# Four-layer graph network: six of sixteen neighbour lists made between layer 0's weighings, node products within the first lists, table rows of 520, anchored lists

## The chip, the cores and the metric

The kernel runs on one core of a Trainium2 chip. A core has a matrix engine (TensorE, in the profile PE, with its weight loads as PEld), three engines for elementwise work (VectorE or DVE, ScalarE or ACT, GpSimd or POOL), a synchronisation engine (SyncE, SP) that mainly issues transfers, and 16 DMA engines that all queues share. Each engine runs its instructions in order and waits for the others by semaphores. SBUF is the on-chip memory of 128 partitions, PSUM the accumulator of TensorE. The metric is the device time of one execution in microseconds; the times given are the median of runs without a profile.

## The reference

The input is x of 8 batches, 2048 nodes and 64 features, and one adjacency matrix for all batches, symmetric, with the diagonal set and some 9 entries in a row. Four layers each compute x = layernorm(x + layer(x, adj)). Cut to what matters here:

```python
# layer 0: graph attention with a LeakyReLU of a sum of two scores
h = layernorm((x * node_weights + node_bias + x) @ W) * gamma + beta
s1, s2 = h @ a1, h @ a2
e = leaky_relu(s1[:, :, None] + s2[:, None, :], 0.2)
att = softmax(where(adj > 0, e, NEG), axis=-1)
x = layernorm(x + elu(att @ h + h))
# layer 1: attention per feature, softmax of feat * wa over the neighbours
# layer 2: mean of the neighbours, two products, relu, layernorm
# layer 3: four dot-product attention heads over h = x Wh, then one over their joined output
```

Only about 9 of 2048 entries of each row count, so the kernel works on lists of edges.

## The kernel before, in words

Nodes are cut into 16 tiles of 128. A tile has NG = 2 groups of 64 nodes, and each group's edges are laid into GS = 5 slots of 128 places, filled from the group's two ends inwards: nodes 0 to 31 forwards, 32 to 63 backwards. WINDOWS (line 69) says which nodes of a group may have edges in which slot; since degrees are random, the windows overlap. For each tile the kernel makes `SelT` and `Sel` (which place belongs to which node, and its turn) and `src` (which node's row each place must fetch). A gather is one indirect DMA, issued by GpSimd, that fetches 128 rows of a table in DRAM by `src`; a tile takes ten (L204, helper `gather`).

**List phase** (the loop at L364 on). For each tile the adjacency rows are loaded by SP (`load`), turned into marks and counted on ScalarE (`on`, L368), for the first eight tiles also transposed by TensorE into ET (L376, L377); VectorE makes keys (L370), takes the largest eight of each 256 (L380), merges them to 24 neighbours (L385, L387); TensorE sums the degrees of the nodes in front (`before`, L396), VectorE makes offsets and, with ScalarE's `apart` (L405), `SelT` (L406); ten products and two copies make `Sel` (L411 to L415), seven instructions make `src` (L419 to L427). After each second list `node_products` does two tiles of h = x W: transposes (L127), products with W (L301) and with the attention vectors (L303), a square on ScalarE (L306), reduction (L307), an inverse root in some twelve small instructions (L142 to L147), the scaled H (L316). H stays in SBUF for all tiles and is stored to the table `htab0`, rows of 512 (8 batches x 64); a score stands in place of column 0 of W, which the sum of the others restores later. The order of this phase is set by the framework's scheduler.

**Weighing** (manual order, the loop over k that calls fetch, weights, divide, combine, weigh, activate, normalise). Step k gathers tile k+1 into `hs` (two buffers), adds the two scores (`wm`, L461), makes exponentials on ScalarE (L464, L465), multiplies the gathered rows by them (L476, five instructions), sums by node on TensorE (L482, with the denominators `pd`, L484), divides the tile before (`rd`, L490 and ScalarE, L493), and for the tile before that restores the column, applies gamma and beta and adds H (L497 to L500), then ELU and the residual (L502 to L508) and layer norm's statistics for pairs of tiles (L156 to L162); `normed` on ScalarE (L170) applies them.

Layer 1 begins with `f` on ScalarE (L580). Its lists, layer 2's and layer 3's use the same `Sel` and `src`. In layer 3's heads (manual order) a step is one slot of one group: ten gathers to a tile, scores of the slot's 128 rows against the window's nodes (L1101), exponentials (L1104), the edge mask (L1107), sums `po` (L1126). `sides` makes U, the node side of the scores, in two calls for a tile; ScalarE copies head h0 and VectorE head h0 + 1 (L1073, L1074).

Of the kernel before, what the change touches and what calls it, by code (L numbers as in the profile page):

```python
# [48 lines left out]
def kernel(ctx: ExitStack, tc: tile.TileContext, ins: dict, out: bass.AP):  # L49
# [19 lines left out]
    WINDOWS = [(0, 20), (10, 32), (20, 44), (32, 54), (44, 64)]  # L69
# [117 lines left out]
    room = main.tile([P, 2], F32, name="room")  # L187

# [35 lines left out]
    htab0 = dram.tile([N + 1, BD], F32, name="htab0")  # L224
    no_row(htab0)
    l0 = ExitStack()
    wp = l0.enter_context(tc.tile_pool(name="l0w", bufs=1, reuse_waits="tile"))
    H = wp.tile([P, NT, BD], F32, name="H")
# [4 lines left out]
    aps = adj_.enter_context(tc.tile_pool(name="adjps", bufs=2, space=PSUM, reuse_waits="tile"))  # L233
# [5 lines left out]

    ats = {0: load(0)}  # L240
    a1 = rows("a1", ins["L0_gnn_a"].rearrange("f o -> (f o)")[0:D], wp)
# [20 lines left out]
    for k, a in enumerate((a1, a2)):  # L262
# [5 lines left out]
        if k:  # L268
            first_col = wp.tile([P, 2], F32, name="first_col")
            nc.vector.tensor_copy(first_col, Wv[:, :, 0])  # L270
            nc.vector.tensor_copy(Wv[:, :, 0], Wa[:, 1])
            nc.vector.tensor_copy(Wa[:, 1], first_col)

# [13 lines left out]
    def node_products(t0, wk, ps):  # L287
# [4 lines left out]
        for q in range(HALF):  # L292
# [12 lines left out]
            sq = wk.tile([P, B, D], F32, name="sq")  # L305
            nc.scalar.activation(sq.rearrange("p b d -> p (b d)"), ph.rearrange("p a n -> p (a n)"), AF.Square)  # L306
            nc.vector.tensor_reduce(var[:, q], sq[:, :, 1:], AX.X, ALU.add)  # L307
            held.append(ph)
        v4, r4, t4 = (a.rearrange("p q (a k) -> p q a k", k=2) for a in (var, rstd, tmp))
        nc.vector.tensor_tensor(t4, pq[:, :, :, 1], pq[:, :, :, 1], ALU.mult)  # L310
        nc.vector.tensor_tensor(var, var, tmp, ALU.add)
        nc.vector.scalar_tensor_tensor(var, var, 1.0 / D, eps.unsqueeze(2).to_broadcast(var.shape), op0=ALU.mult, op1=ALU.add)
        inv_sqrt(*(a.rearrange("p q b -> p (q b)") for a in (rstd, var, tmp)))
        for q, ph in enumerate(held):
            t = t0 + q
            nc.vector.tensor_tensor(H[:, t].rearrange("p (b d) -> p b d", d=D),  # L316
                                    ph.rearrange("p a (k d) -> p (a k) d", d=D), along(rstd[:, q]), ALU.mult)
            nc.sync.dma_start(htab0[t * P:(t + 1) * P, :], H[:, t])
# [33 lines left out]
    base = aw.tile([P, 1], F32, name="base")  # L352
    nc.vector.tensor_scalar(base, part[:, 3:4], float(GB), float(GE), op0=ALU.is_ge, op1=ALU.mult)

# [9 lines left out]
    for it in range(NT):  # L364
        at = ats.pop(it) if it in ats else load(it)
        nc.scalar.dma_start(X[:, it], x[:, it * P:(it + 1) * P, :].rearrange("b p d -> p b d"))
        on = ap_.tile([P, N], BF16, name="on")
        nc.scalar.activation(on, at, AF.Sign, bias=minus_half, accum_out=deg[:, it:it + 1])  # L368
        key = ap_.tile([P, N], F16, name="key")
        nc.vector.tensor_tensor(key, on, from_end, ALU.mult)  # L370
        nc.vector.tensor_scalar(deg[:, it:it + 1], deg[:, it:it + 1], 0.5, 0.5 * N, op0=ALU.mult, op1=ALU.add)
        for c in range(NCH if it < DENSE else 0):
            pt = aps.tile([P, TPC, P], F32, name="pt")
            for k in range(TPC):
                j0 = (c * TPC + k) * P
                nc.tensor.matmul(pt[:, k], on[:, j0:j0 + P], ident_bf, start=True, stop=True)  # L376
            nc.scalar.activation(ET[:, c * TPC:(c + 1) * TPC, it * P:(it + 1) * P], pt, AF.Relu, saturate=False)  # L377
        tops = ap_.tile([P, N // SEG, 8], F16, name="tops")
        for k in range(N // SEG):
            nc.vector.max(tops[:, k], key[:, k * SEG:(k + 1) * SEG])  # L380
        topf = tops.rearrange("p k m -> p (k m)")

        nbr = ap_.tile([P, SL + 1], F16, name="nbr")
        for k in range(0, SL, 8):
            nc.vector.max(nbr[:, k:k + 8], topf)  # L385
            if k + 8 < SL:
                nc.vector.match_replace(topf, nbr[:, k:k + 8], topf, 0.0)  # L387
        junk = ap_.tile([P, P], BF16, name="junk")
        nc.vector.scalar_tensor_tensor(junk, on[:, it * P:(it + 1) * P], 1.0, ident_bf, op0=ALU.mult, op1=ALU.mult,
                                       accum_out=own_edge[:, it:it + 1])  # L390
        nc.vector.scalar_tensor_tensor(junk[:, 0:SL], nbr[:, 0:SL], 0.0, nbr[:, 0:SL], op0=ALU.is_gt, op1=ALU.logical_and,
                                       accum_out=listed[:, it:it + 1])

        plist = aps.tile([P, 2 * CW], F32, name="pl", bufs=1)
        poff = plist[:, 0:1]
        nc.tensor.matmul(poff, before, deg[:, it:it + 1], start=True, stop=True)  # L396
        nc.vector.tensor_scalar(offs[:, it:it + 1], poff, -1.5 * GE, 2.0 * GE, op0=ALU.max, op1=ALU.min)
        nc.vector.tensor_tensor(offs[:, it:it + 1], offs[:, it:it + 1], base, ALU.add)
# [6 lines left out]
        nc.scalar.activation(apart, node_half, AF.Abs, scale=2.0, bias=ends[:, it:it + 1])  # L405
        nc.vector.tensor_scalar(SelT[:, it], apart, deg[:, it:it + 1], None, op0=ALU.is_lt, saturate=False)  # L406
        pl = plist[:, 1:1 + GS * NG * (SL + 1)].rearrange("p (g l) -> p g l", l=SL + 1)
        ps = plist[:, CW // 2:CW // 2 + GE].rearrange("p (s n) -> p s n", n=P)
        for s in range(GS):
            sel = SelT[:, it, s * P:(s + 1) * P]  # L410
            nc.tensor.matmul(pl[:, s * NG:(s + 1) * NG], sel, nbrs, start=True, stop=True)  # L411
            nc.tensor.matmul(ps[:, s], sel, ident_h, start=True, stop=True)
        for k in range(GN // GB):
# [3 lines left out]
                                 AF.Copy, saturate=False)  # L417
        at_ = ap_.tile([P, GS, NG], F32, name="at_")
# [9 lines left out]
        if it % HALF == HALF - 1:  # L428
            node_products(it - HALF + 1, ap_, aps)
    adj_.close()  # L430
# [4 lines left out]
    wk = l0.enter_context(tc.tile_pool(name="l0k", bufs=2, reuse_waits="tile"))  # L435
    ps_e = l0.enter_context(tc.tile_pool(name="l0pse", bufs=2, space=PSUM, reuse_waits="tile"))
    ps_o = l0.enter_context(tc.tile_pool(name="l0pso", bufs=3, space=PSUM, reuse_waits="tile"))
    ps_w = l0.enter_context(tc.tile_pool(name="l0psw", bufs=1, space=PSUM, reuse_waits="tile"))
    held, zs, stats = {}, {}, {}

    def fetch(it):
        hs = wk.tile([P, GS * NG, B, D], F32, name="hs")
        for s in range(GS):
            for g in range(NG):
                gather(hs[:, s * NG + g].rearrange("p b d -> p (b d)"), htab0, it, s, g)
        selTf = wk.tile([P, GE], F32, name="selTf")
# [6 lines left out]
        pe = ps_e.tile([P, GS, NG * B], F32, name="pe")  # L453
        for s in range(GS):
            nc.tensor.matmul(pe[:, s], selTf[:, s * P:(s + 1) * P], s1g.rearrange("p g b -> p (g b)"), start=True, stop=True)  # L455
        held[it] = hs, self_, pe

    def weights(it):
        hs, self_, pe = held[it]
        wm = wk.tile([P, GS * NG, B], F32, name="wm")  # L460
        nc.vector.tensor_tensor(wm, pe.rearrange("p s (g b) -> p (s g) b", b=B), hs[:, :, :, 0], ALU.add)  # L461
# [4 lines left out]
        held[it] = hs, self_, w, wm  # L466

    def weigh(it):
        hs, self_, w, wm = held[it]
        po = ps_o.tile([P, BD], F32, name="po")  # L470
        pd = ps_w.tile([P, B], F32, name="pd")
        for n, ss in enumerate(TOGETHER):
            for s in ss:
                own = slice(s * NG, (s + 1) * NG)
                wx = hs[:, own].rearrange("p g b d -> p (g b) d")
                nc.vector.tensor_tensor(wx, wx, along(w[:, own].rearrange("p g b -> p (g b)")), ALU.mult)  # L476
# [10 lines left out]
    def divide(it):  # L487
# [4 lines left out]
        for b in range(B):  # L492
            nc.scalar.activation(z[:, b], z[:, b], AF.Copy, scale=rd[:, b:b + 1])  # L493
# [1678 lines left out]
```

## Time and profile before

| | us |
|---|---|
| median of 3 runs (1674.72 to 1679.46) | 1674.98 |
| the profiled execution, its own time | 1810.59 |
| its span in the profile | 1808.8 |

Busy time by stage of the profiled execution, in us (the stages' limits are read from the timeline):

| stage | from, to | TensorE | VectorE | ScalarE | GpSimd | clock | DMA share |
|---|---|---|---|---|---|---|---|
| lists and node products | 0, 182 | 98.4 | 149.5 | 106.0 | 4.1 | 0.69 | 0.44 |
| first gathers | 182, 200.5 | 4.4 | 0.4 | 1.0 | 11.7 | 0.50 | 0.60 |
| weighing | 200.5, 452.9 | 133.5 | 195.5 | 105.1 | 141.5 | 0.68 | 0.53 |
| layer 1 | 452.9, 712 | 224.3 | 157.2 | 111.4 | 134.5 | 0.94 | 0.54 |
| layer 2 | 712, 955 | 177.3 | 150.6 | 127.2 | 128.5 | 0.87 | 0.44 |
| layer 3, heads | 955, 1446 | 447.9 | 321.0 | 274.1 | 169.3 | 0.98 | 0.56 |
| layer 3, last attention | 1446, 1808 | 292.6 | 221.7 | 180.7 | 193.4 | 0.87 | 0.58 |

The clock is the share of full speed that TensorE was granted; DMA share is the mean busy share of the 16 DMA engines. In rows of groups the numbers are busy time, mean ns of one, then idle time of the engine just before and what ended it. In a timeline a row has its start, length, engine, line, operation and shapes, and in brackets the idle time before it with what ended it.

### The profile page before, as it was taken

To read this page: it belongs to the slowest core of one execution; us is meant where nothing else is said; L and a number is where in the kernel's file an instruction comes from. 1 tells how busy PE (TensorE), PEld (TensorE's weight loads), DVE (VectorE), ACT (ScalarE), POOL (GpSimd) and SP (SyncE) were. 2 spreads that over 40 slices of the span, in tenths; PEclk is the share of its full clock that TensorE was granted. 3 is DMA by queue.
4 is the path that set the end of the run, shared out by engine and by line. 5 is a ranking of instruction groups with operands and counts; after the bars stand their busy time and mean duration, and the time that the engine had idled before them with its cause. 6 is when DMAs were issued, how large, how long until landed. Compare 5 with 4: busy or idle time off the path is not lost.

```text
span 1808.8 us, 39940 instructions
## 1 busy us (share of the span) xinstructions
PE 1378.3 (76%) x16028; PEld 949.9 (53%) x16028; DVE 1195.8 (66%) x2973; ACT 905.6 (50%) x1863; POOL 782.8 (43%) x777
## 2 busy tenths in 40 slices
PE   4673455653489996888937999999999779889993
PEld 3662233331133332732216777777777657667773
DVE  5989378787576465754763666666667626656667
ACT  5763133535961233535653556555655424555564
POOL 0000666662464552656624333334334056656551
PEclk9665667666799998999967999999999969998897
DMA  6550665552126883256614656665656266666651
GB/s 185 184 160 24 182 179 175 174 175 60 70 105 214 305 309 126 94 153 177 184 46 119 160 155 164 161 160 156 170 155 165 76 198 171 186 179 176 182 152 44
DMA packets 157019, 280.71 MB, mean 155 GB/s; under 512 B 68732, under 2 KB 94332, under 8 KB 154748
## 3 DMA queue, kind: packets, MB, share of 16 engines
q0 software_dynamic: 56320, 189.44, 35.5%
q1 hardware_dynamic: 83866, 84.45, 15.8%
q10 hardware_dynamic: 16640, 4.20, 1.0%
q8 instruction: 128, 2.10, 0.5%
q14 instruction: 65, 0.53, 0.1%
HBM read 237.60 MB, written 40.42 MB: 154 GB/s over the span
## 4 chain that ended last, share of the span: by engine, by line
PE 48%; ACT 8%; DVE 7%; issue 5%; DMA 1%; another core or an unknown queue 1%; POOL 1%; SPq 0%; ACTq 0%; POOLq 0%; DVEq 0%
PE pscore L1101 9%; PE pa L605 6%; PE po L1126 5%; PE ps L1429 5%; PE po L1468 4%; PE pt L1406 3%; PE pa L660 2%; PE pt L713 2%; ACT w L1104 2%; PE pa L1003 2%; PE pscore L1064 2%; PE py L833 2%; PE pe L1399 2%; PE pscore L1193 2%; ACT xsT L1088 1%
## 5 line engine op out<-in xcount | busy, mean ns | idle before, releaser
L204 POOL DMA_INDIRECT xs<-xtab,src x160 | 172.9, 1081 | 282.0 <-PE po L1126 243.9
L204 POOL DMA_INDIRECT hs<-htab,src x160 | 153.1, 957 | 261.7 <-PE pe L455 182.9
L204 POOL DMA_INDIRECT hs<-ktab,src x160 | 158.6, 992 | 139.4 <-DMA utab<-hT 46.3
L605 PE MATMUL pa<-R,ET 128*128 128x512 bf16 x768 | 179.4, 390 | 49.9 <-POOL R L593 33.7
L1107 DVE SCALAR_TENSOR_TENSOR w<-w,Sel 128x640 f32<-128x640 f32 (+2 forms) x160 | 134.2, 875 | 104.7 <-ACT w L1104 104.5
L1104 ACT ACTIVATE w<-pscore 128x640 f32<-128x640 f32 (+2 forms) x160 | 113.6, 745 | 145.5 <-PE pscore L1101 139.9
L1101 PE MATMUL pscore<-U,xsT 64*128 64x80 f32 (+2 forms) x2560 | 163.6, 278 | 5.4 <-DVE U L1074 4.3
L605 PEld LDWEIGHTS <-ET 128*128 128x128 fp8e4 x768 | 74.7, 100 | 162.5 <-issue 83.3
L170 ACT ACTIVATE X<-X,ln_m,ln_r 128x64 f32<-128x64 f32 x256 | 87.2, 427 | 144.3 <-DVE ln_m L162 134.0
L1101 PEld LDWEIGHTS pscore<-U,xsT 64*128 64x128 f32 x2560 | 152.6, 191 | 11.6 <-DVE U L1074 6.9
L1126 PE MATMUL po<-w,xs 128*64 128x88 f32 (+2 forms) x3072 | 130.8, 237 | 14.4 <-DVE w L1107 5.3
L1126 PEld LDWEIGHTS po<-w,xs 128*64 128x64 f32 x3072 | 113.8, 139 | 48.0 <-DVE w L1107 25.6
L1468 PE MATMUL po<-hs,w 128*32 128x65 f32 x2048 | 87.3, 234 | 33.2 <-issue 25.3
L1429 PE MATMUL ps<-U,hsT 128*128 128x64 f32 x768 | 104.3, 287 | 9.0 <-ACT hsT L1407 4.8
L1429 PEld LDWEIGHTS ps<-U,hsT 128*128 128x128 f32 x768 | 102.8, 210 | 10.0 <-ACT hsT L1407 5.4
L204 POOL DMA_INDIRECT rs<-rtab,src x80 | 75.8, 948 | 63.4 <-PE pa L660 43.0
L614 DVE RECIPROCAL rec<-pa 128x256 f32<-128x256 f32 x32 | 54.4, 1734 | 64.6 <-PE pa L660 30.8
L1468 PEld LDWEIGHTS po<-hs,w 128*32 128x32 f32 x2048 | 70.8, 118 | 45.0 <-issue 33.4
L1407 ACT COPY hsT<-pt 128x512 f32<-128x512 f32 x96 | 52.5, 586 | 81.8 <-remote 46.4
L476 DVE TENSOR_TENSOR hs<-hs,w 128x1024 f32<-128x1024 f32 x80 | 91.8, 1213 | 1.2 <-ACT wm L464 0.4
L204 POOL DMA_INDIRECT rs<-ytab,src x80 | 76.9, 961 | 32.9 <-issue 17.1
L1516 ACT ACTIVATE z<-z,ln_m,ln_r 128x64 f32<-128x64 f32 x240 | 83.4, 432 | 14.7 <-DVE ln_m L1504 14.1
(634 smaller groups left out, 3087.4 us busy)
## 6 DMA issues: line engine op xcount, KB each, us to landing
at<-in_adj SPq DMA_DIRECT2D x16, 1024.0 KB
R<-itab SPq DMA_DIRECT2D x60, 256.0 KB
rtab<-r SPq DMA_DIRECT2D x16, 512.0 KB
ptab<-hp SPq DMA_DIRECT2D x16, 384.0 KB
hi<-ptab SPq DMA_DIRECT2D x16, 384.0 KB
ktab<-hb SPq DMA_DIRECT2D x16, 260.0 KB
X<-in_x ACTq DMA_DIRECT2D x16, 256.0 KB
htab<-H SPq DMA_DIRECT2D x16, 256.0 KB
```

Source lines behind the costliest of these rows:

```text
L170: nc.scalar.activation(v[:, b], v[:, b], AF.Identity, scale=rstd[:, k:k + 1], bias=nmr[:, k:k + 1])
L204: nc.gpsimd.indirect_dma_start(out=dst, out_offset=None, in_=table[:, :], in_offset=bass.IndirectOffsetOnAxis(ap=src[:, it, s, g:g + 1], a ...
L476: nc.vector.tensor_tensor(wx, wx, along(w[:, own].rearrange("p g b -> p (g b)")), ALU.mult)
L605: nc.tensor.matmul(po[h].rearrange("p a f -> p (a f)"), ET[:, jt, it * P:(it + 1) * P], R[:, jt, q, h].rearrange("p a f -> p (a f)"), star ...
L614: nc.vector.reciprocal(rec, po[h][:, 0])
L1101: nc.tensor.matmul(pscore[:, k_, f0:f0 + HN * ni].rearrange("p (h i) -> p h i", i=ni), xsT[half, p], Us[it][half, p, :, i0:i0 + ni], start ...
L1104: nc.scalar.activation(w.rearrange("p k a h i -> p k (a h i)"), pscore[:, :, 0:NP * HN * ni], AF.Exp)
L1107: nc.vector.scalar_tensor_tensor(wt, wt, 3.0e38, edge, op0=ALU.min, op1=ALU.mult)
L1126: nc.tensor.matmul(po[half, p, :, a - blk * GB:b - blk * GB], xs[:, f0:f0 + D], w[:, k_, p, :, a - WINDOWS[s][0]:b - WINDOWS[s][0]], start ...
L1429: nc.tensor.matmul(pscore[:, g, 2 * p:2 * p + 2], hsT[:, g, p], U[:, p, :, node_block(g, k)], start=False, stop=(p == NP - 1))
L1468: nc.tensor.matmul(po[node_block(g, k), j, b], w[:, g, t], hs[:, g, t], start=(s == BEGIN[k] and b == 0), stop=(s == END[k] and b == B // ...
L1516: nc.scalar.activation(v, v, AF.Identity, scale=r, bias=n)
```

## The change

The lists of tiles 0 to 9 are made first, as before; those of tiles 10 to 15 are cut into small parts (`mark`, `count`, `make_keys`, `top_of`, `neighbours`, `tests`, `places`, `select`, `edges`, `sources`), which `between` puts into the weighing's steps 0 to 12, one list in two steps. All node products come with the first eight lists, two tiles with each, and x is loaded two tiles to a list. The table's rows grow to 520: eight scores stand behind the 512, so that column 0 needs no restoring. GpSimd multiplies H by gamma before it is stored, and adds beta for a second table `own0`, from which SP loads a tile's own rows again in the weighing. `hs` gets three buffers, `combine` follows one step behind. Lists are anchored: two more masks (`far`) and shifts give nodes from 16 and from 28 on, counted from a group's ends, a least place of 128 and 256, so that the windows are 16, 18, 32, 18 and 16 wide instead of 20, 22, 24, 22 and 20; the offset is the maximum of three sums. In layer 3 the middle slot's weights have a buffer of their own, and U is copied by halves of the batches.

```diff
-    WINDOWS = [(0, 20), (10, 32), (20, 44), (32, 54), (44, 64)]
+    ANCHORS = (16, 28)
+    WINDOWS = [(0, 16), (10, 28), (16, 48), (36, 54), (48, 64)]
...
-    htab0 = dram.tile([N + 1, BD], F32, name="htab0")
+    htab0 = dram.tile([N + 1, BD + B], F32, name="htab0")
+    own0 = dram.tile([N, BD], F32, name="own0")
...
-            nc.vector.tensor_reduce(var[:, q], sq[:, :, 1:], AX.X, ALU.add)
+            nc.vector.tensor_reduce(var[:, q], sq, AX.X, ALU.add)
...
-        nc.vector.tensor_tensor(t4, pq[:, :, :, 1], pq[:, :, :, 1], ALU.mult)
-        nc.vector.tensor_tensor(var, var, tmp, ALU.add)
...
-            nc.vector.tensor_tensor(H[:, t].rearrange("p (b d) -> p b d", d=D),
-                                    ph.rearrange("p a (k d) -> p (a k) d", d=D), along(rstd[:, q]), ALU.mult)
-            nc.sync.dma_start(htab0[t * P:(t + 1) * P, :], H[:, t])
+            H = wk.tile([P, BD + B], F32, name="H")
+            Hv = H[:, 0:BD].rearrange("p (b d) -> p b d", d=D)
+            nc.vector.tensor_tensor(Hv, ph.rearrange("p a (k d) -> p (a k) d", d=D), along(rstd[:, q]), ALU.mult)
+            nc.vector.tensor_tensor(H[:, BD:].rearrange("p (a k) -> p a k", k=2), pq[:, q, :, 1], r4[:, q], ALU.mult)
+            nc.gpsimd.tensor_tensor(Hv, Hv, over(g0, Hv.shape), ALU.mult)
+            nc.sync.dma_start(htab0[t * P:(t + 1) * P, :], H)
+            Hb = wk.tile([P, B, D], F32, name="Hb")
+            nc.gpsimd.tensor_tensor(Hb, Hv, over(b0, Hv.shape), ALU.add)
+            nc.sync.dma_start(own0[t * P:(t + 1) * P, :], Hb.rearrange("p b d -> p (b d)"))
...
+        for k in range(3):
+            nc.tensor.matmul(poff[:, k:k + 1], ident_bf, shift_bf[:, k:k + 1], start=True, stop=False)
+            nc.tensor.matmul(poff[:, k:k + 1], outer[k], deg[:, it:it + 1], start=False, stop=True)
...
+        nc.vector.tensor_reduce(far_off, poff, AX.X, ALU.max)
+        nc.vector.tensor_scalar(offs[:, it:it + 1], far_off, 2.0 * GE, depth[:, 1:2], op0=ALU.min, op1=ALU.mult)
...
-        if it % HALF == HALF - 1:
-            node_products(it - HALF + 1, ap_, aps)
+    AHEAD = 10
+    for it in range(AHEAD):
+        for t in range(2 * it + 2, min(2 * it + 4, NT)):
+            load_x(t)
...
+        if it < NT // HALF:
+            node_products(it * HALF, prk, prps)
+    products.close()
...
-        hs = wk.tile([P, GS * NG, B, D], F32, name="hs")
+        hs = rk.tile([P, GS * NG, BD + B], F32, name="hs", bufs=3)
...
+    def prepare(it):
+        own = wk.tile([P, B, D], F32, name="own")
+        nc.sync.dma_start(own.rearrange("p b d -> p (b d)"), own0[it * P:(it + 1) * P, :])
...
     def combine(it):
-        z = zs[it]
-        nc.vector.tensor_tensor(z, z, H[:, it].rearrange("p (b d) -> p b d", d=D), ALU.add)
-        nc.vector.tensor_reduce(z[:, :, 0], z[:, :, 1:], AX.X, ALU.add, negate=True)
-        nc.vector.tensor_tensor(z, z, over(g0, z.shape), ALU.mult)
-        nc.vector.tensor_tensor(z, z, over(b0, z.shape), ALU.add)
+        z, own = zs[it]
+        nc.vector.tensor_tensor(z, z, own, ALU.add)
...
+    def between(k, place_):
+
+        it, odd = AHEAD + k // 2, k % 2
+        if it < NT:
+            if (odd, place_) == (0, 3):
+                mark(it)
+            if (odd, place_) == (0, 2):
+                count(it)
+                make_keys(it)
+                top_of(it, 0, 4)
+            if (odd, place_) == (1, 0):
+                top_of(it, 4, N // SEG)
+            if (odd, place_) == (1, 1):
+                neighbours(it)
+                tests(it)
+                places(it)
+            if (odd, place_) == (1, 2):
+                select(it)
+                edges(it)
+        if (odd, place_) == (0, 0) and it - 1 in lists:
+            sources(it - 1)
+        if (odd, place_) == (1, 2) and it + 1 < NT:
+            ats[it + 1] = load(it + 1)
...
             if k < NT:
                 weights(k)
+            between(k, 0)
             if 1 <= k <= NT:
                 divide(k - 1)
-            if 2 <= k <= NT + 1:
-                combine(k - 2)
+            if k + 1 < NT:
+                prepare(k + 1)
             if k < NT:
-                weigh(k)
-            if 2 <= k <= NT + 1:
-                activate(k - 2)
+                weigh(k, 0, 1)
+            if k + 1 < NT:
+                scores(k + 1)
+            between(k, 1)
+            if 1 <= k <= NT:
+                combine(k - 1)
+            between(k, 3)
+            if k < NT:
+                weigh(k, 1, 2)
+            if 1 <= k <= NT:
+                activate(k - 1)
+            between(k, 2)
+            if k < NT:
+                weigh(k, 2, 3)
...
-            U = Us[it].rearrange("p (j a) h n -> p j a h n", j=2)
-            nc.scalar.copy(U[:, :, :, h0], pu[:, :, 0])
-            nc.vector.tensor_copy(U[:, :, :, h0 + 1], pu[:, :, 1])
+            U = Us[it].rearrange("p (j a) h n -> p j a h n", j=2)[:, :, :, h0:h0 + 2]
+            nc.scalar.copy(U[:, 0], pu[:, 0].rearrange("p h a n -> p a h n"))
+            nc.vector.tensor_copy(U[:, 1], pu[:, 1].rearrange("p h a n -> p a h n"))
...
-            w = ws[k] = wk.tile([P, 2, NP, HN, ni], F32, name="w", bufs=4)
+            w = ws[k] = wk.tile([P, 2, NP, HN, ni], F32, name="w_mid" if s == MID else "w", bufs=1 if s == MID else 4)
...
+            nc.vector.tensor_scalar(ends, ends, meet[:, 0:1], None, op0=ALU.mult)
+            nc.vector.scalar_tensor_tensor(ends, offs, meet[:, 1:2], ends, op0=ALU.mult, op1=ALU.add)
```

In the changed file H's product stands in L320, its row tail in L321, the two products that end `node_products` in L327 and L328.

## The prediction

> **What bounds the kernel now.** I read the busy time by stages, then the timelines of VectorE and GpSimd around layer 0, then the groups by shape of the two stages whose shapes change. In the stage view the columns are length, busy time of TensorE, its weight loads, VectorE, ScalarE and GpSimd, granted clock, DMA share, GB/s.
>
> ```profile
> 45.00:90.00 45.00, 30.88 (x222) 27.75 (x222) 41.28 (x201) 33.45 (x59) 0.00 (x0) 0.67 0.54 183
> 270.00:315.00 45.00, 24.93 (x182) 14.11 (x182) 37.44 (x79) 17.39 (x54) 28.68 (x30) 0.77 0.59 173
> ```
>
> The first row is the list phase: VectorE is busy 92% and GpSimd idle. The second is the weighing phase: GpSimd's 30 gathers fill three steps of about 14.5 us, VectorE has 83%, TensorE half. Between the two lies a hole.
>
> ```profile
> 182.14 0.25 DVE L451 TENSOR_TENSOR s1g<-S,group 128x16 f32<-128x16 f32 x2
> 200.54 0.28 DVE L461 TENSOR_TENSOR wm<-pe,hs 128x80 f32<-128x80 f32 x1 [18.15 <-DMA hs<-htab,src]
> ```
>
> VectorE waits 18.15 us, because gathers may start only when the last table row is written, and that row is the list phase's last work. Inside the weighing:
>
> ```profile
> 222.61 0.95 POOL L204 DMA_INDIRECT hs<-htab,src  x1 [0.30 <-issue]
> 227.14 0.95 POOL L204 DMA_INDIRECT hs<-htab,src  x1 [2.32 <-PE pe L455]
> 409.25 0.69 DVE L498 TENSOR_REDUCE po<-po 128x8 f32<-128x504 f32 x1
> 409.97 0.70 DVE L499 TENSOR_TENSOR po<-po,g 128x512 f32<-128x512 f32 x1
> 410.71 0.70 DVE L500 TENSOR_TENSOR po<-po,b 128x512 f32<-128x512 f32 x1
> 411.31 5.73 DVE L476 TENSOR_TENSOR hs<-hs,w 128x1024 f32<-128x1024 f32 x5
> ```
>
> A step is ten gathers at 1.26 us (0.96 and 0.30 between two), 12.6, and about 2 us in which GpSimd waits for one of the two hs buffers. The three small rows go with the change. First `wm` 200.54, second 213.22, sixteenth 422.27: the weighing's pitch is 14.9. Layer 1's first `f` starts at 450.6. The chain of waits lists no long piece before 528 us, so for this stage the timelines decide.
>
> **What the skill says.** The Trainium skill, "SBUF — State Buffer", section "Who interferes with whom": VectorE with two SBUF inputs and GpSimd reading SBUF exclude each other, and the later one blocks until the first is done. The trace agrees; in layer 1 a 1.21 us instruction starts behind a GpSimd one, and ends 1.1 us after it:
>
> ```profile
> 540.45 2.12 POOL L597 TENSOR_TENSOR R<-rest,R 128x1024 bf16<-128x1024 f32 x1
> 540.52 3.13 DVE L595 TENSOR_TENSOR rest<-r,R 128x1024 f32<-128x1024 f32 x1 [0.93 <-POOL R L593]
> ```
>
> "GPSIMD Engine Reference", "3.1 Elementwise — side-by-side cycle accounting", has a two-input GpSimd product about twice as slow as VectorE's; here 1.264 us (L908, 512 elements) against 0.69. "TensorE: Matmul & The Clock Gate", "LDWEIGHTS (loading the stationary operand)": a load's cost goes by its columns. That fits what the head stage shows, where the score product doesn't follow its moving width but `po` does:
>
> ```profile
> L1101 PE MATMUL pscore<-U,xsT 64*128 64x80 f32 x1000 | 68.8, 278 | 4.3 <-DVE U L1074 4.3
> L1101 PE MATMUL pscore<-U,xsT 64*128 64x96 f32 x496 | 33.5, 275 | 0.0
> L1126 PE MATMUL po<-w,xs 128*64 128x88 f32 x1008 | 52.3, 246 | 1.4 <-DVE w L1107 1.4
> L1126 PE MATMUL po<-w,xs 128*64 128x48 f32 x1024 | 36.8, 225 | 2.2 <-DVE w L1107 1.8 <-issue 0.2
> ```
>
> **The change, part by part.** *List phase.* Ten lists stay ahead of the weighing; the first eight each carry two tiles of node products. Now, list 3 to 15 start (L368) at 40.67 to 156.74: 9.67 us each; VectorE's busy time is (149.5 − 6.8 before 20 us)/16, say 8.8. A product tile's share: reduction and H at 0.60 each, half of fifteen small ones at 0.09, is 1.9; so a list is 6.9, a turn with two tiles 10.6. TensorE: 6.15 on average now, 1.0 for a list that is also transposed, 3.6 for a second product tile (its three lines sum to 4.7, cut to 78% because the lines' sums exceed the engine's total so), 1.3 for five more offset products: 12. ScalarE about 9. New on GpSimd: four 128x512 products a turn (gamma, beta), 1.27 each. In the emitted order VectorE's two-input instructions L321, L327, L328 and `ends` stand right behind H. Four GpSimd instructions take 5.6 us with their gaps; between them VectorE gets through about 1.5 us of work; it loses 4.1. So (10.6 + 4.1) and the tenth that waits add today: 16 us a turn. Bounds for the block: 0 and 5.6. The reduction, copies and L310/L311 that go, and the row tail and maximum that come, cancel.
>
> Key 0, at 18.33 now, stands behind some 27 added small instructions (0.07 to 0.28): 22. Key 1 comes 6.5 later as now; eight turns: key 9 at 156.5; list 9's chain, 12 as in list 15 now: 168.5. The last H stands two thirds into the last turn, 151.2; three GpSimd products 4.2; issue and write 3.2 (181.95 to 185.20 now), the last store of own0 1.4: gathers start at 160, hidden behind lists 8 and 9. First `wm` after the 15.3 of now: 175. Against 200.5: −25.5.
>
> *Weighing.* hs has three buffers: the 2 us wait goes, and GpSimd's floor is 12.6. Queues: X loads move forward on ScalarE's, 0.37 each; SP gets 32 stores more, 16 loads of own and the last adjacency loads; own is issued a step or more before it is read, adjacency two lists ahead, so I cost them nothing; if late, VectorE stalls at `combine`. DMA: gathers 0.6 × 14.5 = 8.7 us a step, own 0.26 MB and half an adjacency tile 0.5 MB at 3.4 us/MB (queue 1: 285 us for 84.45 MB) 2.6: 11.3.
>
> VectorE, without the three rows: a step without statistics is now 10.4 (`wm` at 407.94 to the end of the second X instruction, 418.3), less 2.05 is 8.35; the statistics of a pair (eight bn_stats and twelve small ones, 402.98 to 407.05) are 4.1, on even steps. A list adds on even steps: count 0.07, keys 1.14, four maxima 1.34, sources 1.86 (five instructions, each waiting for the one before); on odd steps: maxima 1.34, neighbours 1.32, tests 0.5, places 0.85, SelT 0.5. Even 17, odd 13. Added waits: on odd steps the second list's products follow SelT on TensorE; behind them ScalarE does two copies to Sel and eight normalisations (2.65), and behind these stand the next exponentials, for which `hs` waits. SelT end plus 6.0 against VectorE's own 4.5, with waits for `pl` (0.5) and division (0.3): 2.4 on each even step. A pair: 32.4.
>
> Second `wm` is bounded by gathers: 187.6. Step 1: 13; steps 2 to 11: 162; step 12: 16.9; 13: 9.7; 14: 13.8. Sixteenth `wm`: 403 (now 422.3). So six lists cost 6.4 us here. *End:* combine follows one step behind, not two: 9.7 to the last `hs`, 2 TensorE, 2.7 division, 0.7, 0.7, 1.4 and part of the statistics: `f` 19.3 after `wm` (28.3 now): 422.3. **Against 450.6: −28.3.**
>
> *Heads.* Windows sum to 100 nodes, not 108. `po`: slope (51.9 − 35.9)/40 = 0.4 ns per column, 8 nodes × 4 heads × 16 instructions × 32 = 6.6 us less. Score: flat to 96 columns; the middle one goes to 128, not shown: bound 0 to +7, taken +3.6. `U` by halves: ScalarE and VectorE write apart, TensorE's 4.3 us wait for U: −2 taken, 0 to −6. Exponentials of the wide window are later, VectorE absorbs it at 65% busy. Together −5, from −12 to +5. The two instructions for the final tests: under 0.4, nothing.
>
> Sum: 1810.6 − 33.3 = 1777.3 for the profiled execution (span 1808.8). The median shown is 0.925 of it; in proportion: **1644 us**.
>
> **Rivals.** (a) *GpSimd hardly blocks* (its products run while VectorE has one-input work): turns of 13.3, 22 us less: 1623. For: MAX8 has one input; against: L321, L327 stand next to H. (b) *The gain is partly given back*: a list step near 17.5 as TensorE, at half clock, delays SelT's products and so the exponentials: 1.3 × 12 = 16: 1659. (c) *Slower*, one mechanism: ScalarE's order. The exponentials stand behind Sel and normalisation; if that wait is 9 us a pair and not 2.4, the pair is 38 to 39, six pairs lose 37 and the gain is gone; beyond 39 it is slower, at 41 about 1690. Against: ScalarE has some 9 busy us of 16. (d) *The heads take all the gain or nothing*: only ±8. (e) The change doesn't do what it says, gathers still waiting for the last of the ten lists: they start at 168.5 + 3.2 and the last stalls as now, 12 to 25 us later, at most 1667; against: the emitted order has all H before list 9's neighbours.
>
> **From here to the numbers.** Forecast 45% (own range 1628 to 1658), (a) 24%, (b) and (e) 14%, no change 6%, (c) 11%. Below 0.3%, 5 us, a measurement can't tell. Faster 0.83, same 0.06, slower 0.11. The range reaches from (a)'s middle with 14 us of room for turns of 12.5 and the heads' −12, to (e) with room: 1608 to 1672; the rest of (a), and (c), is left out.
>
> **What would show it.** Key instructions 16 us apart in the first eight turns, and L321, L327, L328 lasting 1 us or more beside GpSimd products; first gather near 160, first `wm` near 175; the weighing's GpSimd no longer waiting for `pe`/`pd`, even steps about 19, odd 13; first `f` near 422. In the heads, 128-column scores at 68 ns pitch. Wrong it goes if turns stay near 13, if `hs` waits on ScalarE's exponentials for over 5 us, or if gathers land late.

## The result and the profile after

Changed kernel: 1652.6 us, median of 4 runs (1650.1 to 1659.0), beside 1676.8 for the kernel before (1674.7 to 1679.5): 0.986 of the time before, 95% interval 0.983 to 0.990, 24 us. Forecast 1644, range 1608 to 1672.

One thing has to be known to read the numbers. The runs were made on several chips: on one, here chip A, the kernel before takes 1677 us, on two others, B and C, 1828 and 1817. The 1652.6 was measured beside a kernel before of A's speed and is counted to A, though its chip is not noted; the profile of before that the prediction read (1810.6) has the speed of B and C, though its median has that of A. Comparisons below stay within a chip or use ratios to the kernel before on the same chip; where they don't, the text says so.

Three words are used throughout. A turn is one round of the list phase with a list and two tiles of node products, measured from one key instruction to the next. A step is one tile of the weighing, measured from `wm` to `wm`; a pair is two steps.

The profile of the changed kernel (its own time 1659.0, span 1657.2). First the stage view, with columns as in the prediction:

```profile
45.00:90.00 45.00, 35.53 (x209) 31.90 (x207) 41.09 (x157) 24.34 (x47) 14.83 (x13) 0.54 0.56 184
270.00:315.00 45.00, 29.33 (x188) 16.73 (x190) 41.66 (x117) 22.87 (x65) 25.03 (x27) 0.54 0.59 177
```

In the list phase (first row) TensorE's busy time is 79% now, at a clock of 0.54, and GpSimd has work. In the weighing (second row) VectorE is busy 93%, and GpSimd 25 us of 45. The timeline:

```profile
159.57 1.13 POOL L206 DMA_INDIRECT hs<-htab,src  x1 [2.92 <-DMA own<-Hb]
174.77 0.24 DVE L565 TENSOR_TENSOR wm<-pe,hs 128x80 f32<-128x80 f32 x1 [5.79 <-DMA hs<-htab,src]
313.30 0.94 POOL L206 DMA_INDIRECT hs<-htab,src  x1 [6.25 <-PE pe L587]
327.11 2.35 DVE L580 TENSOR_TENSOR hs<-hs,w 128x1024 f32<-128x1024 f32 x2 [0.74 <-ACT w L569]
394.87 0.23 DVE L565 TENSOR_TENSOR wm<-pe,hs 128x80 f32<-128x80 f32 x1
413.70 2.91 ACT L720 ACTIVATE f<-X,bb,w 128x512 f32<-128x512 f32 x4
```

First gather at 159.57, first `wm` at 174.77 after a wait of 5.8 us (18.2 before), sixteenth at 394.87, layer 1's first `f` at 413.70. GpSimd waits 6 us in each pair of steps until a buffer comes free. The heads, by shape (busy time, mean ns, idle before):

```profile
L1241 PE MATMUL pscore<-U,xsT 64*128 64x64 f32 x1024 | 71.3, 278 | 4.7 <-issue 3.6 <-ACT xsT L1228 1.1
L1266 PE MATMUL po<-w,xs 128*64 128x72 f32 x1024 | 45.0, 231 | 0.5 <-DVE w L1247 0.5
L1266 PE MATMUL po<-w,xs 128*64 128x64 f32 x1024 | 44.0, 229 | 5.2 <-DVE o L1250 4.5 <-DVE w L1247 0.7
L1266 PE MATMUL po<-w_mid,xs 128*64 128x64 f32 x1024 | 36.9, 225 | 3.8 <-DVE w_mid L1247 3.5
L1241 PE MATMUL pscore<-U,xsT 64*128 64x128 f32 x512 | 36.6, 284 | 0.0
```

The 128-column scores take 71.5 ns each (36.6/512); those of 96 columns took 69.3 in the kernel before on A (35.5/512). New is a wait of 3.5 us for `w_mid`, which has one buffer.

### The profile page after: what moved, and what is told of

Its sections match the earlier page's. It is cut to its first block, busy times and chain, and to the rows that moved or that the text cites. A ratio compares the mean times of both kernels' runs of the same rounds, so it can differ in the third digit from the quotient of the medians.

```text
span 1657.2 us, 40196 instructions
## 1 busy us (share of the span) xinstructions
PE 1346.4 (81%) x16140; PEld 928.4 (56%) x16140; DVE 1191.5 (72%) x2947; ACT 905.2 (55%) x1863; POOL 815.7 (49%) x810
## 4 chain that ended last, share of the span: by engine, by line
PE 46%; DVE 12%; ACT 5%; issue 4%; POOL 3%; DMA 1%; SPq 0%; POOLq 0%; ACTq 0%; DVEq 0%
PE pscore L1241 9%; PE pa L745 6%; PE po L1266 6%; PE pscore L1204 4%; PE pt L853 3%; PE pa L800 3%; PE ps L1569 3%; PE po L1608 2%; PE py L973 2%; PE pscore L1333 2%; PE pt L1546 2%; PE pa L1143 1%; ACT z L1010 1%; POOL hs L206 1%; ACT X L1010 1%
## 5 line engine op out<-in xcount | busy, mean ns | idle before, releaser
L1241 PE MATMUL pscore<-U,xsT 64*128 64x64 f32 (+2 forms) x2560 | 163.7, 278 | 4.7 <-issue 3.6
L1244 ACT ACTIVATE w<-pscore 128x512 f32<-128x512 f32 (+1 forms) x128 | 79.7, 623 | 92.5 <-PE pscore L1241 91.9
L1247 DVE SCALAR_TENSOR_TENSOR w<-w,Sel 128x512 f32<-128x512 f32 (+1 forms) x128 | 92.4, 723 | 40.3 <-ACT w L1244 37.3
L754 DVE RECIPROCAL rec<-pa 128x256 f32<-128x256 f32 x32 | 54.1, 1730 | 63.8 <-PE pa L800 38.0
L1569 PE MATMUL ps<-U,hsT 128*128 128x64 f32 x768 | 96.5, 273 | 1.5 <-ACT hsT L1547 1.5
L1569 PEld LDWEIGHTS ps<-U,hsT 128*128 128x128 f32 x768 | 95.2, 197 | 1.8 <-ACT hsT L1547 1.7
L1266 PEld LDWEIGHTS po<-w,xs 128*64 128x64 f32 x2048 | 71.1, 139 | 32.0 <-issue 17.5
L1143 PE MATMUL pa<-Y,ET 128*128 128x512 bf16 x384 | 88.7, 380 | 0.0
L1266 PE MATMUL po<-w,xs 128*64 128x64 f32 (+1 forms) x2048 | 83.8, 230 | 5.8 <-DVE o L1250 4.5
L1228 ACT COPY xsT<-pt 128x1024 f32<-128x1024 f32 x80 | 81.0, 1012 | 10.5 <-PE pt L853 10.2
L1608 PE MATMUL po<-hs,w 128*32 128x65 f32 x2048 | 73.7, 226 | 4.6 <-DVE w L1581 4.6
```

What stands on the lines that cost most here:

```text
L1143: nc.tensor.matmul(sums[it], ET[:, jt, it * P:(it + 1) * P], Y[:, jt, q].rearrange("p a n -> p (a n)"), start=(jt == 0 and q == 0), stop=( ...
L1228: nc.scalar.copy(unflipped(xsT), pt.rearrange("p k s a n -> p k (s a) n"))
L1241: nc.tensor.matmul(pscore[:, k_, f0:f0 + HN * ni].rearrange("p (h i) -> p h i", i=ni), xsT[half, p], Us[it][half, p, :, i0:i0 + ni], start ...
L1247: nc.vector.scalar_tensor_tensor(wt, wt, 3.0e38, edge, op0=ALU.min, op1=ALU.mult)
L1266: nc.tensor.matmul(po[half, p, :, a - blk * GB:b - blk * GB], xs[:, f0:f0 + D], w[:, k_, p, :, a - WINDOWS[s][0]:b - WINDOWS[s][0]], start ...
L1569: nc.tensor.matmul(pscore[:, g, 2 * p:2 * p + 2], hsT[:, g, p], U[:, p, :, node_block(g, k)], start=False, stop=(p == NP - 1))
```

## Experiments

**The kernel before, a second time** (chip A).

> The kernel before, unchanged, for a second profile, because in the first one (own time 1810.6) the heads took 491 us and the last attention 362, against 450 and 297 in the changed kernel, although the last attention's code is the same in both. Theory A: the first profile was disturbed from the heads on, and layer 0 in it was as always: now about 1680 in all, first wm at 200, first f of layer 1 at 450. Then layer 0 gained 37 us (first f at 413.7 in the changed kernel), more than the 24 of the whole, and other stages lost some 13. Theory B: its weighing was disturbed as well: first f at about 437, layer 0's gain is about the whole gain and nothing else moved.

1675.35 us. Its stage view and timeline:

```profile
270.00:315.00 45.00, 26.19 (x200) 15.38 (x194) 41.60 (x89) 23.32 (x72) 32.75 (x35) 0.69 0.68 201
262.92 0.95 POOL L204 DMA_INDIRECT hs<-htab,src  x1 [2.16 <-PE pd L484]
305.36 0.28 DVE L461 TENSOR_TENSOR wm<-pe,hs 128x80 f32<-128x80 f32 x1
317.82 0.28 DVE L461 TENSOR_TENSOR wm<-pe,hs 128x80 f32<-128x80 f32 x1 [1.42 <-issue]
332.59 0.28 DVE L461 TENSOR_TENSOR wm<-pe,hs 128x80 f32<-128x80 f32 x1
427.37 2.21 ACT L580 ACTIVATE f<-X,bb,w 128x512 f32<-128x512 f32 x3
```

Theory A fell, B was nearer (it said f at 437). Here steps take 14.8 and 12.5 us in turn, 13.3 in the mean (199.2 to 399.0), and VectorE is busy 92%; in the first profile 14.9 and 83%. GpSimd's 2 us wait is still there, but VectorE is full in the same steps, and the sums for which GpSimd waits stand behind VectorE's products. So, between these two profiles, layer 0 gains 427.4 − 413.7 = 13.7 us: 24.5 at the first `wm` (199.2 to 174.8), 9.5 at the end (from the last `wm` to `f` 28.3, now 18.8), and it gives back 20.3 in the weighing (199.8 to 220.1), where VectorE's busy time rises from 170.0 to 197.5. The two spans differ by 16.3 us and not by the medians' 24, since the profiled execution of the changed kernel was the slowest of its four. Layer 0's end is steady: in the next two versions, on A too, `f` starts at 413.5 and 414.5.

**Heads undone** (A).

```diff
-    ANCHORS = (16, 28)
-    WINDOWS = [(0, 16), (10, 28), (16, 48), (36, 54), (48, 64)]
+    ANCHORS = (64, 64)
+    WINDOWS = [(0, 20), (10, 32), (20, 44), (32, 54), (44, 64)]
...
-            nc.scalar.copy(U[:, 0], pu[:, 0].rearrange("p h a n -> p a h n"))
-            nc.vector.tensor_copy(U[:, 1], pu[:, 1].rearrange("p h a n -> p a h n"))
+            nc.scalar.copy(U[:, :, :, h0], pu[:, :, 0])
+            nc.vector.tensor_copy(U[:, :, :, h0 + 1], pu[:, :, 1])
...
-            w = ... name="w_mid" if s == MID else "w", bufs=1 if s == MID else 4)
+            w = ... name="w", bufs=4)
```

> The changed kernel with the five old windows (anchors set so far out that they never hold, the same instructions), the U copies by heads and one buffer set for the weights of all slots: the heads' part of the change undone. The forecast's step 'heads -5' says: 5 us slower than the changed kernel, 0.989 to 0.990 of before. The rival from the whole against layer 0's gain says that the heads lost about 13 us: then 13 us faster than the changed kernel, 0.978 of before.

0.991 of before (0.989 to 0.993) against 0.986: the heads' part is worth 0.0049 × 1677, some 8 us, and the rival, a loss of 13, fell. (The four runs, 1661.3 to 1667.2, also lie wholly above those of the next version, measured together with it: 1653.1 to 1657.8.) From the first edge mask to the last `o` the trace shows 2.9 us (915.8 to 1338.1 undone, 915.9 to 1335.3 changed). Most of the rest of this profile's lag lies between the last `o` and the last attention's first `z` (60.8 us here, 55.5 in the changed kernel, 54.1 before), single executions that I can't explain.

**U by heads** (A): the two U lines of the last diff alone.

> The changed kernel with only the U copies by heads again. The forecast's term of -2 for the copies by halves says 2 us slower than the changed kernel, 0.987 of before, and in the heads a wait of TensorE for U of about 4 us as before; if the halves cost something, it is faster than the changed kernel by what they cost.

0.987 (0.985 to 0.989): not to be told from the changed kernel. TensorE's 4.7 us wait for `U` is back in the trace, so the copies by halves take the wait away; the time does not show what that is worth.

**No scaling in the node products** (A).

```diff
-            nc.gpsimd.tensor_tensor(Hv, Hv, over(g0, Hv.shape), ALU.mult)
...
-            nc.gpsimd.tensor_tensor(Hb, Hv, over(b0, Hv.shape), ALU.add)
-            nc.sync.dma_start(own0[t * P:(t + 1) * P, :], Hb.rearrange("p b d -> p (b d)"))
+            nc.sync.dma_start(own0[t * P:(t + 1) * P, :], H[:, 0:BD])
```

> The changed kernel without the products with gamma and the sums with beta in layer 0's node products (left out; H itself goes into both tables), so GpSimd does nothing in the list phase. The forecast's step 'the block on VectorE costs 4.1 us of a turn of 16' says: turns of 12, first gather at about 125 to 130 instead of 160, first wm 142 to 148, about 28 us faster than the changed kernel, 0.97 of before. The rival: turns are set by TensorE's products at half clock and by ScalarE behind them (VectorE waits 2.4 us a turn for the marks): turns of 15 or more, 8 us faster at most, 0.981 of before or more.

0.982 (0.980 to 0.984): the rival. In the changed kernel the block is there. The first three rows are from VectorE's timeline beside GpSimd's products, the fourth is from the end of the same turn, and the last two, of ScalarE, are from just before the end of the next one:

```profile
86.98 0.15 DVE L321 TENSOR_TENSOR H<-pq,h_r 128x8 f32<-128x8 f32 x1
87.65 0.77 DVE L321 TENSOR_TENSOR H<-pq,h_r 128x8 f32<-128x8 f32 x1
88.57 1.20 DVE L328 TENSOR_TENSOR S<-h_t,cs 128x16 f32<-128x16 f32 x1
94.88 0.15 DVE L408 TENSOR_SCALAR deg<-deg 128x1 f32<-128x1 f32 x1 [2.40 <-ACT on L404]
108.93 0.17 ACT L308 COPY pq<-pa__1216 128x16 f32<-128x16 f32 x1 [1.96 <-PE pa__1216 L307]
109.00 2.00 ACT L404 ACTIVATE on<-at,minus_half 128x2048 bf16<-128x2048 int32 x1
```

The second tail takes 0.77 instead of 0.15, and L328 1.20 (0.16 without scaling); but at the end of the turn VectorE waits 2.4 us for the marks `on`. ScalarE makes them only after it has waited for TensorE's attention products `pa` and copied them. Without scaling:

```profile
93.61 0.15 DVE L405 TENSOR_SCALAR deg<-deg 128x1 f32<-128x1 f32 x1 [3.69 <-ACT on L401]
109.86 0.15 DVE L405 TENSOR_SCALAR deg<-deg 128x1 f32<-128x1 f32 x1 [3.69 <-ACT on L401]
```

The turn is still 16.25 us; VectorE only waits longer. Taking 5 us of work a turn from GpSimd left the turns in the middle as they were, so the block did not set them. The first gather comes at 152.75, 6.8 earlier, and `f` at 406.96, 6.7 earlier: the last H is made 4.0 us sooner (147.40, 151.39), because turns at the two ends got shorter (13.1 instead of 15.2 after key 1, and the last three by 5.2 together), and its way to the first gather is 2.8 us shorter without the products. So the block costs some 4 us in all eight turns, not 4.1 in each.

**Masks in 16 bits** (B, then C): the masks and the counts of the offset products as 16-bit floats, exact for these numbers.

```diff
+    for k in range(3):
+        mask_h = aw.tile([P, P], F16, name=f"mask_h{k}")
+        nc.vector.tensor_copy(mask_h, outer[k])
+        outer[k] = mask_h
...
+        deg_h = ap_.tile([P, 1], F16, name="deg_h")
+        nc.vector.tensor_copy(deg_h, deg[:, it:it + 1])
...
-            nc.tensor.matmul(poff[:, k:k + 1], outer[k], deg[:, it:it + 1], start=False, stop=True)
+            nc.tensor.matmul(poff[:, k:k + 1], outer[k], deg_h, start=False, stop=True)
```

> The changed kernel with the three masks of the offset products and the counts in 16-bit floats (exact for these numbers; three small copies in the setup and one of 128x1 a list come on top). If TensorE at half clock paces the first eight turns (its products fill 13.5 of 16.2 us there, and taking GpSimd's work away left the turn at 16.2), three products of 0.57 us become some 0.2 us shorter to 0.1 each: 1 to 1.3 us less a turn, first gather at 150 to 152 instead of 159.6, 7 to 9 us faster than the changed kernel, 0.981 of before. If the chain of ScalarE's marks and VectorE's small work paces it, nothing is gained, 0.986.

> The masks in 16-bit floats again, beside the changed kernel on the same chip. The list phase alone gave first gather at 151.6 instead of 159.6. If VectorE sets the whole weighing, these 8 us arrive at the end: 0.9815 of before at 1676 us, 7 to 9 us faster than the changed kernel. If gathers or TensorE's stops set it, less than 3 us arrive.

B: 0.994 (0.992 to 0.996); C: 0.993 (0.991 to 0.995), where the changed kernel has 1.000. First the changed kernel's stage view over one turn (chip A, 94.90 to 111.15; on C a turn has the same 16.25, 13.46 and clock 0.50), then that of half masks over one turn on B and one on C:

```profile
94.90:111.15 16.25, 13.45 (x75) 12.19 (x76) 13.83 (x53) 9.00 (x18) 5.01 (x4) 0.50 0.50 164
```

```profile
77.00:92.00 15.00, 12.21 (x73) 10.94 (x74) 13.79 (x54) 8.95 (x18) 5.01 (x4) 0.50 0.55 175
86.52:100.28 13.76, 10.58 (x76) 9.12 (x73) 13.74 (x55) 9.04 (x18) 5.02 (x4) 0.62 0.59 193
```

On B, at the same clock of 0.50, TensorE's busy time falls by 1.2 us and the turn by 1.25: what the edit takes from TensorE comes off the turn. On C the clock is 0.62 as well (3.4 us of full clock in each turn, while `pa` is made), busy time is 10.58, and the turn is 13.76, which VectorE now fills to 13.74. VectorE's and ScalarE's instructions are the same but for one small copy. So TensorE's order was what set 16.2, through ScalarE, whose marks stand behind the products' results. The sum of TensorE's busy time alone doesn't set it: the changed kernel's turn from 62.60 to 78.74 on A had a clock of 0.61 and only 12.28 us busy, and still took 16.14; its full clock fell at the start of the turn, ahead of this chain.

On B the first gather comes at 151.6, as expected (159.6 in the version with two buffers there, whose list phase is the changed kernel's). On C it comes at 144.6 against 160.8 in the changed kernel on the same chip, first `f` at 441.9 against 457.3, and the median is 12.9 us less (1805.5, 1818.3): nearly all of it arrives, more than I expected. Set beside B, about half of these 16 us at the first gather is the clock's. This version is faster than both kernels on C; on A it was not run, and on B the changed kernel was not run.

**All sixteen lists ahead** (B, then C).

```diff
-    AHEAD = 10
+    AHEAD = 16
```

> The changed kernel with all sixteen lists ahead of the weighing and none between; all else as changed. The forecast's idea that lists between the weighings cost little there (six for 6.4 us) says: six lists at some 8.8 us come ahead, little comes back, 30 us or more slower than the changed kernel, 1.005 of before. The rival: VectorE does the same work in either place and is the bound in both, first wm at about 222, then steps of 12.6 by GpSimd's gathers with three tiles fetched ahead, last wm at about 397 (394.9 in the changed kernel): 2 us slower, 0.987.

> All sixteen lists ahead again, beside the changed kernel. VectorE as the bound: about 2 us slower than the changed kernel on a chip with before at 1676 (0.987). The forecast's idea that lists between the weighings cost only 6.4 us: 30 us or more slower (1.005). On a chip with before at 1827 it was 1.008, with first wm at 232.8 and steps of 15 without any list in them.

B: 1.008 (1.005 to 1.011). C: 1.010 (1.007 to 1.012), 17 us slower than the changed kernel there: between the two expectations. On C the first `wm` is at 233.9 (176.1 changed), the sixteenth at 454.8 (438.5), so the six lists cost 57.8 ahead and 41.5 between. But VectorE stands still twice in these 57.8, while the first 30 gathers run:

```profile
188.06 0.17 DVE L491 TENSOR_TENSOR at__1768<-place,pl 128x10 f32<-128x10 f32 x1 [10.20 <-issue]
202.24 0.16 DVE L450 TENSOR_REDUCE far_off<-pl 128x1 f32<-128x3 f32 x1 [11.09 <-remote]
```

Without these 21.3 us the lists would have cost 36.5 ahead, less than between; so this run does not show what they cost ahead on A, where no such stops were found. The steps, with no list in them, no three rows and three buffers, take 14.7 us, no less than the 14.8 of the first profile of before (200.5 to 422.3). So, on this kind of chip, neither the rows nor the buffer was what made that pitch.

**Twelve ahead**, four between (B); the same with half masks (C).

```diff
-    AHEAD = 10
+    AHEAD = 12
```

> Twelve lists ahead and four between. By the rival above, VectorE's waits for the first gathers (5.8 and 3.8 us in the changed kernel) are filled with a list, and the last four steps have nothing but weighing: first wm at about 184, last wm at 386 to 390, 5 to 8 us faster than the changed kernel, 0.982. By the forecast's idea 10 us slower, 0.992.

> Half masks with twelve lists ahead and four between. If VectorE is the bound, two lists more ahead fill its wait for the first gathers: 4 to 6 us faster than half masks alone (0.978 of before at 1676). If TensorE's stops beside the gathers are the bound, it is slower than half masks alone by about 10, as twelve ahead was (1.003) on the slower chip.

1.003 (1.002 to 1.005) on B, where the changed kernel was not run; half masks have 0.994 there. With half masks on C 0.995 (0.994 to 0.997), 4.6 us slower than half masks alone on the same chip, `f` at 449.2 and not 441.9, though the two intervals overlap. No gain on these chips, and on B probably a loss; for A, where VectorE is the bound, it stays open.

**Two hs buffers** (B).

```diff
-        hs = rk.tile([P, GS * NG, BD + B], F32, name="hs", bufs=3)
+        hs = rk.tile([P, GS * NG, BD + B], F32, name="hs", bufs=2)
```

> The changed kernel with two hs buffers instead of three. The forecast's step 'three buffers take away GpSimd's wait of 2 us a step' says that the steps without lists at least get 2 us longer, and pairs go from 31 to 33 or more: 15 to 30 us slower, 0.995 to 1.003 of before. The rival: VectorE alone sets the pair (about 30 of 31 us busy), the buffer is spare: within 3 us, 0.986 to 0.988.

0.991 (0.989 to 0.994): faster, where the changed kernel has 1.000 on C. That compares two chips; half masks' ratio agrees between B and C to 0.001, and on B itself two buffers are 6.7 us faster than half masks with three (1812.2, 1818.9), though their first gather comes 8 us later. Neither expectation had that sign. The next run shows where the time goes.

**The changed kernel on C.**

> The changed kernel, unchanged, as the reference beside the three others on one chip: 0.986 of before where before takes some 1676 us. Where before takes some 1827 us (as on the chip of the four runs before these), the timelines there have TensorE standing still for 1 to 3 us between single products while gathers run, in both kernels; layer 0 then gains little (first f at about 450 in both), the heads' gain stays: 0.991 to 0.994.

1818.3 against 1816.7: 1.000 (0.998 to 1.002), no change; the expected 0.991 to 0.994 is missed. First `f` is at 457.3, later than the 450.6 of the first profile of before. TensorE's timeline in its first step, then VectorE's:

```profile
185.62 0.18 PE L412 MATMUL pl<-shift_bf,ident_bf 128*128 128x1 bf16 x1
186.84 0.16 PE L413 MATMUL pl<-deg,before 128*128 128x1 f32 x1 [1.04 <-issue]
188.25 0.16 PE L413 MATMUL pl<-deg,before 128*128 128x1 f32 x1 [1.25 <-issue]
190.34 0.16 PE L412 MATMUL pl<-shift_bf,ident_bf 128*128 128x1 bf16 x1 [1.93 <-issue]
193.14 0.16 PE L413 MATMUL pl<-deg,far 128*128 128x1 f32 x1 [2.63 <-issue]
202.24 2.69 PE L586 MATMUL po<-hs,self__1750 128*32 128x512 f32 x7 [0.54 <-issue]
```

```profile
202.99 0.24 DVE L565 TENSOR_TENSOR wm<-pe,hs 128x80 f32<-128x80 f32 x1 [17.54 <-remote]
```

The six offset products, 0.9 us of work on A (182.24 to 183.1 there), take 16 here: each stands alone, with gaps in which the engine waits for nothing that the profile shows ("issue"), and VectorE waits 17.5 us for something that the profile doesn't name ("remote"). The step from the first to the second `wm` is 27 us. With two buffers GpSimd stops after tile 1's gathers until 191.3, and the stops end at 188:

```profile
187.25 0.16 PE L413 MATMUL pl<-deg,before 128*128 128x1 f32 x1 [1.24 <-issue]
188.00 0.57 PE L413 MATMUL pl<-deg,far 128*128 128x1 f32 x2
189.00 0.24 DVE L565 TENSOR_TENSOR wm<-pe,hs 128x80 f32<-128x80 f32 x1 [4.71 <-remote]
```

That step is 14.1 us; on the same chip with three buffers (the half masks) 27.1. A third buffer lets 30 gathers run without a pause, and on B and C the stops end when they are done: the last packet of these gathers lands at 201.1 in the changed kernel on C, and `wm` starts at 202.99; with two buffers on B the packets pause from 188.2. It is not TensorE alone: in the run with all lists ahead on C, above, VectorE waited 11 us for `far_off`, whose product TensorE had ended at 190.8, and went on at 202.24, 2 us after the last packet. Over the whole weighing VectorE's waits of over 0.45 us without a name add up to 41.8 us on C and to 3.8 on A; the weighing is 42.3 us longer (262.4, 220.1) at nearly the same busy time (198.7, 197.5). On A 30 gathers run without a pause too, and TensorE has no such gap there, in either kernel. The profile of before that the prediction read has 19 on TensorE, 17 us in all, beside the wait for the first tile: its speed could be seen in it.

What stops the engines is not settled: the queues of instructions moved two packets between 160 and 204 (three on A in the same stretch), so late instructions can't be read from it, nor ruled out.

## The prediction, step by step

*List turns, 16 us: the sum right, the reason wrong.* Keys 1 to 6 came 15.2 to 16.3 us apart, the next three 13.8, 19.4 and 11.2; key 0 at 21.2 (22), key 9 at 155.6 (156.5), gathers at 159.6 (160), first `wm` at 174.8 (175). Key 9 was met by two errors that cancel: key 1 came 10.7 after key 0 and not 6.5, and the eight turns after it took 123.6 and not 128. (On paper, (149.5 − 6.8)/16 is 8.9 and not 8.8.) But of 10.6 + 4.1 + a tenth, the 4.1 for the block was no term of the turn: leaving GpSimd's products out changed nothing in the middle turns. TensorE, costed at 12 and set aside, is busy 13.45 of 16.25; 1.2 us less of it took the turn to 15.0, and with a higher clock it came to 13.8. The two reasons gave the same total by chance. The Trainium skill, "SBUF — State Buffer", "Who interferes with whom", was right that the block exists; whether it costs depends on the engine having no other wait in the same round.

*Weighing: the step that was wrong.* "hs has three buffers: the 2 us wait goes", and, resting on it, "six lists cost 6.4 us here". On A, where the result was measured, the pitch to be compared with was 13.3, not 14.9, with VectorE at 92%, and the lists' net cost was 20.3 and not 6.4: lists and sources are VectorE's work, which rose by 27.5 us although the three rows went. (No run on A takes the third buffer or the lists away alone; there the account rests on the two profiles.) The sum for the new kernel was near: second `wm` 188.0 (187.6), pairs of 30.2 to 31.1 (32.4), the exponentials' wait 0.7 and not 2.4 on an even step, sixteenth `wm` 394.9 (403). So the new kernel was costed by its instructions, the old one by a profile from a slower chip, and the difference of the two was the error: 28.3 us forecast for layer 0, 13.7 found. On the kind of chip that the profile came from, the third buffer even cost time.

*End.* From the last `wm` to `f` 18.8 (19.3): right.

*Heads, −5:* right in sign, and in size between the trace's −3 and the ratio's −8. Terms: `po` −10.9 us of TensorE's time and not −6.6 (136.8 on A before: 51.9, 49.2, 35.7; now 45.0, 44.0, 36.9), because the middle slot's 48 to 64 columns cost 223 and 225 ns: flat, where I had taken the slope. The wide score cost 1.1 (35.5 to 36.6 on A) and not 3.6. `w_mid`'s 3.5 us and 3.3 us more for `o` (4.5, 1.2 before) gave a part back, and were not foreseen.

*In proportion.* 1777 was scaled by 0.925. The true factor differs by stage: between the first profile and that of A, first `wm` 200.5 and 199.2, the weighing 221.7 and 199.8. On the kind of chip of the profile the changed kernel took 1818, not 1777. The median's range held because on A layer 0's gain was halved, not lost, and by the ratio the heads gave more than forecast. That the time was measured on A, and not on a chip like that of the profile, was luck.

*Rivals.* (b), steps near 17.5 because SelT's products come late, has the number that B and C show, but not its reason: on C pairs are 34 to 35 us, and ScalarE's copies to Sel wait 49 us in the weighing (26 on A); but this comes with the stops, and the clock is about that of A (0.58 and 0.60 over the weighing). (a)'s number fell, turns of 13.3, though its reason was right, since GpSimd hardly costs; (e) fell; (c)'s wait was 0.7 us and not 9; (d) fell, the heads gave about a third.

## What to carry to other kernels

A profile whose own time is 8% above the median is no baseline: take a second one, and add up the waits without a name. Before crediting a wait's removal, see whether another engine is full in the same round. If two engines' chains both explain a round's length, take work from one and then from the other: only the one that moves it pays. More buffers for a gather also mean more traffic without a pause; on two chips of three that went with stops of the engines beside it.

## What had not been expected of the hardware

The six offset products of a list, three of them a 128x128 fp32 mask with one fp32 column, took 1.5 us at a clock of 0.50 (100.51 to 102.05 in the changed kernel on A), in 16 bits 0.35 (64.49 to 64.84 on C, also at half clock). The turn fell by as much on B, and by twice as much on C, where the clock rose as well: the granted clock was 0.50 with TensorE busy 83% of a turn and, on B, 81%, and 0.62 with 77% on C.

One program took 1677 us on one chip and 1817 to 1828 on two others. There TensorE stood still for up to 2.6 us between single products, and VectorE, with a wait that has no name, for 10 to 18 us at a time, while gathers ran, and a change that gained 24 us on the one gained nothing on another.
